# A two-layer graph network: layer 2's attention weights and TensorE sums placed inside the tile in front, with the sums in the residual's PSUM bank

## The chip, the core and the metric

The program runs on one core of a Trainium2 chip. A core has five engines with queues of their own: TensorE (PE; its weight loads are shown as PEld), VectorE (DVE), ScalarE (ACT), GpSimd (POOL) and SyncE (SP). Each works through its own instructions in program order, and engines wait for each other by semaphores. PSUM, the memory that TensorE writes, has eight banks of 512 float32 numbers in each of 128 partitions. The metric is the device time of one execution in microseconds; all arithmetic is in float32.

## The reference, cut to what matters

Two graph attention layers over 10,000 nodes and 170,000 edges (80,000 random ones, their reverses and one loop a node, sorted by destination; the layer then adds a second loop to every node). Layer 1 has 4 heads of 256 columns, layer 2 one head of 768.

```python
def gat_conv(x, edge_index, W, a_src, a_dst, bias, heads, out_ch, concat):
    n = x.shape[0]
    ei = _add_self_loops(edge_index, n)
    src, dst = (ei[0], ei[1])
    xl = (x @ W).reshape(n, heads, out_ch)
    alpha_src = jnp.einsum('nhc,hc->nh', xl, a_src)
    alpha_dst = jnp.einsum('nhc,hc->nh', xl, a_dst)
    e = jax.nn.leaky_relu(alpha_src[src] + alpha_dst[dst], 0.2)
    m = jax.ops.segment_max(e, dst, num_segments=n)
    e = jnp.exp(e - m[dst])
    s = jax.ops.segment_sum(e, dst, num_segments=n)
    alpha = e / (s[dst] + 1e-16)
    msg = xl[src] * alpha[:, :, None]
    out = jax.ops.segment_sum(msg, dst, num_segments=n)
    out = out.reshape(n, heads * out_ch) if concat else out.mean(axis=1)
    return out + bias
...
h0 = x
h = gat_conv(x, edge_index, W1, a_src1, a_dst1, b1, HEADS, HID, True)
h = layer_norm(h, g1, be1)
h = jax.nn.relu(h)
h = h + (h0 @ Wr1 + br1)
h1 = h
h = gat_conv(h, edge_index, W2, a_src2, a_dst2, b2, 1, OUT_DIM, False)
h = layer_norm(h, g2, be2)
h = h + (h1 @ Wr2 + br2)
return h
...
x = _layernorm(x + _L0_gnn_ref(x, edge_index, ...), axis=-1)
```

## The kernel before, in words

Nodes are sorted by degree and cut into 79 tiles of 128 nodes, one node to a partition. A tile has as many *slots* as its largest degree needs: `SLOTS` runs from 8, 9, 10, 11, 11, 11, 12, 12, 12, 13 (five tiles), 14 (five), 15 (eight), 16 (seven), 17 (eight), 18 and 19 (seven each), 20 (six), 21 and 22 (four each), 23, 23, 24, 24, 25, 26, 27 to 41 for the last tile, 1377 in all. In the text n stands for the slots of a tile.

Three stages follow each other. First x @ W1 is written to a table in device memory while the edge lists are prepared. Layer 1 then goes over the tiles, and writes each tile's rows of the layer 2 table (768 columns and two logits) and its h1. Layer 2, `ordered_layer2`, goes over the tiles again; only it is changed.

**The ring.** `Ring.fetch` (called `ring.fetch`) issues one indirect gather on POOL for each slot: 128 table rows of 770 numbers, one to a partition, 394 KB, into one of `RING2` = 40 places used in turn. A place may be filled again when the row in it has been used by DVE and by PE. All gathers go through the helper `gather`, line 409. The loop asks for row k + 40 of its tile right after row k is weighed.

**A tile's work.** `weights_of(t)` (L820 and the helpers `logits`, L454 to L462, and `normalised`, L469 to L475) makes the softmax weights e: adds of logits, maximum and difference on DVE, the exponential on ACT, then the sum, reciprocal and scaling on DVE. It needs every row of the tile to have landed. It is a generator in two halves, before and after the exponential. `sums` (L830 to L837) makes columns 512 to 767 of the weighted sum on PE: a one-row matmul puts the bias in, then for each slot ACT scales the identity by e (a *diagonal*, L836) and PE multiplies it with the row's last 256 columns (L837; a float32 matmul shows as two records). `weigh` (L492) makes columns 0 to 511 with one multiply-add on DVE a slot. `residual(t)` (L846, L848) computes x + h1 @ Wr2 on PE into a tile of two PSUM banks, of which it uses 768 of 1024 columns; `fetch_x` brings h1 (SP, L810) and the rows of x (POOL) for it. The statistics and the scaling by g2 and be2 (`deviation`, L534 to L538, and `scaled`, L547 to L550), the adding of the residual (L874) and the last normalisation follow on DVE; `finish` ends with an ACTIVATE (L884) into the buffer `out`, of which there is one, and a scatter on POOL (L921) sends it to the output rows.

**The order.** The program is emitted by hand in this order, and no scheduler moves it. In the loop for tile t:

- PE and ACT get the sums of tile t, in two halves; between them DVE gets the statistics and scaling of tile t - 1.
- PE gets the residual of tile t + 1 (in the first loop that of tile 0, then `q = product(brT, wr2, C2)`, the shift that br1 makes).
- For k in 0 to n - 1: DVE weighs row k, POOL is given the gather of row k + 40. After row 1 `finish` ends tile t - 1 on DVE and ACT. At n // 2 the inputs of tile t + 2 are asked for. From k = n - 3 (`LEAD` = 3) the two halves of tile t + 1's weights are made, one a row.
- After the last row POOL is given the scatter of tile t - 1.

The last tile, of 41 slots, does not fit in the ring and goes through `attend_parts`: three groups of 13 and 14 rows, all 768 columns on DVE (41 multiply-adds, L492 into `wr`).

PSUM is divided into two buffers `acc` and two `sum` of one bank each, and two residual tiles of two banks: eight banks.

## Time and profile before

| | |
|---|---|
| median of 3 runs | 5635.8 us (5628.9 to 5637.64) |
| the profiled execution | 5634.25 us, span 5632.5 us, mean granted TensorE clock 0.918 |
| first gather of layer 2 | 3570.54 us |
| last scatter | 5627.15 us |
| in 3562 to 5632 us: PE, DVE, ACT, POOL busy | 1674.8, 1636.0, 748.5, 1502.8 us |
| DMA engines in that stretch | busy share 0.90, 316 GB/s |
| POOL over the span | 3411.6 us, 61% |

The profile is one execution. "Busy" counts instructions at work; issuing and waiting are not counted. A timeline row reads: start in us, duration, engine, line, operation, result <- operands, how many merged, and in brackets the idle time of that engine just before, with the instruction or transfer that ended it. A waits row reads: engine, operand and line <- what it waited for: total us, times, longest. `L409 DMA_INDIRECT ring` is POOL's part of one gather; the transfer itself then runs on 16 DMA engines and lands some microseconds after.

### The profile page before, as it was taken

The page shows a single profiled execution, that of the slowest core. Times are in us where ns is not written, and L with a number is a line of the kernel's source. Part 1 is how long each engine was busy: PE and PEld are TensorE (multiplying, and loading weights), DVE is VectorE, ACT ScalarE, POOL GpSimd, SP SyncE. Part 2 cuts the span into 40 slices and gives each one's busy share as a digit, 9 for nine tenths or more (in the row PEclk, how much of TensorE's full clock was granted, in tenths as well). Part 3 has the DMA queues.
Part 4 walks back from the last instruction along what each step waited for, and adds up shares of the span by engine and source line. Part 5 has one row for each costly group of instructions (what it writes and reads, how often), then busy time and mean ns, then how long its engine had stood idle before and what let it go on. Part 6 is the DMA issues. An engine that isn't in the chain of part 4 may idle for free. (4 is left out here: it accounts for less than half of the span.)

```text
span 5632.5 us, 56575 instructions
## 1 busy us (share of the span) xinstructions
PE 4694.2 (83%) x14464; PEld 2762.6 (49%) x14464; DVE 4446.0 (79%) x7881; ACT 3145.5 (56%) x8061; POOL 3411.6 (61%) x3396
## 2 busy tenths in 40 slices
PE   9999997999999998888777654499988888888772
PEld 4444444555555555444444332266556565555551
DVE  5883344788999999999998888388888887877777
ACT  3433444678878888877788766144444343333331
POOL 3446455455556666655655553477777777777773
PEclk9999998999999999999988877799999999888886
DMA  4322427789998999999998876699999999999995
GB/s 155 122 98 80 93 95 263 269 299 327 327 325 324 335 341 332 333 329 326 331 336 320 309 286 225 224 315 330 331 327 332 326 333 324 325 328 330 330 327 163
DMA packets 438659, 1580.90 MB, mean 281 GB/s; under 512 B 102764, under 2 KB 106924, under 8 KB 438327
## 3 DMA queue, kind: packets, MB, share of 16 engines
q0 software_dynamic: 341344, 1400.80, 69.9%
q1 hardware_dynamic: 93168, 170.98, 9.1%
q10 hardware_dynamic: 3814, 5.39, 0.3%
q8 instruction: 122, 2.00, 0.1%
q14 instruction: 211, 1.72, 0.1%
HBM read 1431.10 MB, written 146.19 MB: 280 GB/s over the span
## 5 line engine op out<-in xcount | busy, mean ns | idle before, releaser
L409 POOL DMA_INDIRECT ring<-table,slots x2754 | 2633.6, 956 | 1452.0 <-DVE acc L492 381.5
L492 DVE SCALAR_TENSOR_TENSOR acc<-ring,e,acc 128x256 f32<-128x256 f32 (+1 forms) x2606 | 1609.2, 618 | 134.4 <-PE acc L686 54.5
L481 ACT ACTIVATE ring<-ring,e 128x256 f32<-128x256 f32 x3536 | 1437.1, 506 | 0.0
L488 DVE TENSOR_TENSOR acc<-acc,ring 128x1024 f32<-128x1024 f32 x884 | 1089.1, 1232 | 78.6 <-DVE acc L492 0.9
L837 PE MATMUL sum<-ring,diagonals 128*128 128x256 f32 x2672 | 698.8, 425 | 258.9 <-ACT diagonals L836 256.6
L162 PE MATMUL big<-wr,xT 128*128 128x512 f32 x1896 | 867.4, 616 | 0.7 <-ACT xT L559 0.7
L848 PE MATMUL big<-w,wr 128*128 128x512 f32 (+1 forms) x2528 | 841.0, 485 | 0.0
L162 PE MATMUL big<-w,xT 128*128 128x512 f32 x1896 | 824.8, 597 | 19.1 <-DMA w<-in_W_dram 8.7
L162 PE MATMUL big<-w,hT 128*128 128x512 f32 (+1 forms) x2528 | 833.2, 487 | 1.2 <-ACT hT L559 1.2
L837 PEld LDWEIGHTS sum<-ring,diagonals 128*128 128x128 f32 x2672 | 564.8, 215 | 392.2 <-ACT diagonals L836 296.5
L162 PEld LDWEIGHTS big<-w,hT 128*128 128x128 f32 x2528 | 479.5, 190 | 375.1 <-issue 340.1
L848 PEld LDWEIGHTS big<-w,wr 128*128 128x128 f32 x2528 | 478.4, 189 | 337.0 <-issue 303.2
L162 PEld LDWEIGHTS big<-w,xT 128*128 128x128 f32 x1896 | 362.5, 192 | 478.9 <-issue 461.2
L162 PEld LDWEIGHTS big<-wr,xT 128*128 128x128 f32 x1896 | 371.6, 200 | 441.8 <-issue 440.9
L686 PE MATMUL acc<-ring,diagonals 128*128 128x256 f32 x1248 | 336.0, 430 | 277.8 <-ACT diagonals L681 245.6
L836 ACT ACTIVATE diagonals<-ident,e 128x128 f32<-128x128 f32 x1336 | 420.1, 388 | 124.2 <-PE sum L837 123.0
L884 ACT ACTIVATE out<-wr,less,sd 128x768 f32<-128x768 f32 x79 | 81.1, 1026 | 644.1 <-DMA out_dram<-out,order 556.4
L686 PEld LDWEIGHTS acc<-ring,diagonals 128*128 128x128 f32 x1248 | 269.9, 219 | 338.2 <-ACT diagonals L681 259.9
L634 DVE TENSOR_TENSOR scr<-big,as_b 128x1024 f32<-128x1024 f32 x79 | 96.7, 1225 | 382.3 <-ACT row L631 382.3
L462 ACT ACT_TABLE_LOAD x155 | 198.9, 1283 | 311.1 <-DVE e L461 283.2
L639 POOL TENSOR_TENSOR row<-row,none 128x1024 f32<-128x1024 f32 x79 | 186.9, 2366 | 270.3 <-ACT row L631 269.8
L637 ACT ACTIVATE scr<-scr 128x256 f32<-128x256 f32 x632 | 253.5, 402 | 122.9 <-DVE scr L634 122.9
(171 smaller groups left out, 3938.4 us busy)
## 6 DMA issues: line engine op xcount, KB each, us to landing
ring<-table,slots POOLq DMA_INDIRECT x2754, 5.8
table<-row SPq DMA_DIRECT2D x79, 516.0 KB, 2.9
h_d<-hT SPq DMA_DIRECT2D x79, 512.0 KB, 7.0
wr<-h_d SPq DMA_DIRECT2D x79, 512.0 KB, 6.8
xT<-in_x_cols_dram SPq DMA_DIRECT2D x79, 384.0 KB, 4.3
w<-in_W_dram SPq DMA_DIRECT2D x6, 512.0 KB, 7.3
w<-in_W_dram SPq DMA_DIRECT2D x1, 3072.0 KB, 12.9
wr<-in_Wr_dram SPq DMA_DIRECT2D x1, 3072.0 KB
```

Source lines behind the costliest of these rows:

```text
L162: nc.tensor.matmul(p[:, c:e], aT[:, j, :], w[:, j, c:e], start=(j == 0), stop=(j == k - 1))
L409: nc.gpsimd.indirect_dma_start(out=to, out_offset=None, in_=table, in_offset=bass.IndirectOffsetOnAxis(ap=index, axis=0), **more)
L462: nc.scalar.activation(e, e, AF.Exp)
L481: nc.scalar.activation(row[:, s], row[:, s], AF.Copy, scale=e[:, h:h + 1])
L488: nc.vector.tensor_add(acc[:, :c], acc[:, :c], row[:, :c])
L492: nc.vector.scalar_tensor_tensor(acc[:, s], row[:, s], e[:, h:h + 1], (acc if first is None else first)[:, s], op0=OP.mult, op1=OP.add)
L637: nc.scalar.activation(m[:, s], m[:, s], AF.Copy, accum_out=row[:, C1 + i * H1 + h:C1 + i * H1 + h + 1])
L639: nc.gpsimd.tensor_add(row[:, :C1], row[:, :C1], b1_b)
L686: nc.tensor.matmul(acc[:, c:d], diagonals[:, k * H1 + i, :], ring.slot(FIRST[t] + k)[:, c:d], start=(k == 0 and c % BANK == 0), stop=(k == ...
L836: nc.scalar.activation(diagonals[:, k % G, :], ident, AF.Copy, scale=e[:, k, :])
L837: nc.tensor.matmul(acc, diagonals[:, k % G, :], ring.slot(FIRST[t] + k)[:, ON_PE2:C2], start=False, stop=(k == n - 1))
L848: nc.tensor.matmul(r[:, c:d], hT[:, j, :], wr2[:, j, c:d], start=False, stop=(j == K1 - 1))
```

## The change

Layer 2's loop is written anew with the same operations; helpers are as before.

- The sums on PE become part of `weights_of`: the second half now normalises the weights and then at once makes the tile's diagonals and matmuls. They accumulate into columns 768 to 1023 of the tile's residual, which shares its second bank; so residual(t) has to be issued before. There are no `sum` buffers any more; residual tiles (`big`) become three. Diagonals have `DIAGONALS` = 5 buffers of four instead of two.
- The two halves of tile t + 1's weights are made at row `turn` and three rows later. `turn` is a third of n, or, if more, the row at which the ring has been allowed six rows beyond the end of tile t + 1; at most n - 3.
- `norms` is a generator with the end of tile t - 1 in four pieces, taken in loop t before row 0 (statistics), at row 3 (scaling, residual, statistics), at row 6 (reciprocal, ACTIVATE into `out`) and at row 9 (the scatter on POOL).
- The residual of tile t + 1 is issued at the top of loop t. Residual(0), q and residual(1) come first on PE, ahead of the sums of tile 0; q is added to be2 at the end of loop 0.
- The ring has 38 places instead of 40.

```diff
-RING2 = 40
+RING2 = 38
 LEAD = 3
+DIAGONALS = 5
...
-                tc.tile_pool(name="ps_q2", bufs=2, space=PSUM) as ps_big, tc.manual_schedule():
+                tc.tile_pool(name="ps_q2", bufs=3, space=PSUM) as ps_big, tc.manual_schedule():
...
             def weights_of(t):
...
                 yield e
                 normalised(small, e, H2, t)
+                to = rs[t][:, C2:2 * C2 - ON_PE2]
+                nc.tensor.matmul(to, ones, b2_b[0:1, ON_PE2:], start=False, stop=False, skip_group_check=True)
+                for k in range(n):
+                    if k % G == 0:
+                        diagonals = pool.tile([P, G, P], F32, name="diagonals", bufs=DIAGONALS)
+                    nc.scalar.activation(diagonals[:, k % G, :], ident, AF.Copy, scale=e[:, k, :])
+                    nc.tensor.matmul(to, diagonals[:, k % G, :], ring.slot(FIRST[t] + k)[:, ON_PE2:C2],
+                                     start=False, stop=(k == n - 1), skip_group_check=True)
                 yield
...
+            def norms(t, h, r, means):
+
+                stats = deviation(small, [a for m in means for a in pieces(m, C2 - ON_PE2)])
+                yield
+                scaled(h, means, stats, g2_b, be2_b)
+                nc.vector.tensor_add(h, h, r[:, :C2])
+                mean, inv = deviation(small, pieces(h, C2 // 2))
+                yield
+                nc.vector.reciprocal(inv, inv)
+                less = small.tile([P, 1], F32, name="less")
+                nc.vector.scalar_tensor_tensor(less, mean, -1.0, inv, op0=OP.mult, op1=OP.mult)
+                o = pool.tile([P, C2], F32, name="out")
+                nc.scalar.activation(o, h, AF.Identity, bias=less, scale=inv)
+                yield
+                nc.gpsimd.indirect_dma_start(
+                    out=out, out_offset=bass.IndirectOffsetOnAxis(ap=nodes(t), axis=0),
+                    in_=o, in_offset=None, bounds_check=N - 1, oob_is_err=False)
...
+            rs = {0: residual(0)}
+            q = product(brT, wr2, C2)
+            last = iter(())
...
+            for t in range(NT):
+                n = SLOTS[t]
+                if t + 1 < NT:
+                    rs[t + 1] = residual(t + 1)
+                h = parts[4 + t % 2][:, :C2]
+                if not whole(t):
+                    for _ in last:
+                        pass
...
+                    last = norms(t, h, rs[t], [h])
+                else:
+                    e = (ready or list(weights_of(t)))[0]
                     acc = ps_acc.tile([P, BANK], F32, name="acc")
...
+                    next(last, None)
+                    ready, ahead, turn = [], iter(()), n
+                    if t + 1 < NT and SLOTS[t + 1] + LEAD <= ring.size:
+
                         ahead = weights_of(t + 1)
+                        turn = min(max(n // 3, n + SLOTS[t + 1] + 2 * LEAD - ring.size), n - LEAD)
+                    for k in range(n):
+                        if k in (turn, turn + LEAD):
                             ready += itertools.islice(ahead, 1)
+                        if k in (LEAD, 2 * LEAD, 3 * LEAD):
+                            next(last, None)
                         weigh(acc, ring.slot(FIRST[t] + k), e[:, k], ON_PE2, None if k else b2_b)
                         ring.fetch(FIRST[t] + k + 1 + ring.size)
...
+                    ready += ahead
+                    for _ in last:
+                        pass
+                    if not t:
+                        nc.vector.tensor_add(be2_b, be2_b, q[:, :C2])
+                    last = norms(t, h, rs[t], [acc, rs[t][:, C2:2 * C2 - ON_PE2]])
```

## The prediction

> **What bounds the kernel now.** I read the page's slices and costliest groups first, then the busy times by stage, then GpSimd's waits, and last the timelines of the two ends of layer 2. The page's POOL line and two of its groups:
>
> ```profile
> POOL 3446455455556666655655553477777777777773
> L409 POOL DMA_INDIRECT ring<-table,slots x2754 | 2633.6, 956 | 1452.0 <-DVE acc L492 381.5
> L884 ACT ACTIVATE out<-wr,less,sd 128x768 f32<-128x768 f32 x79 | 81.1, 1026 | 644.1 <-DMA out_dram<-out,order 556.4
> ```
>
> Layer 2 is the last 14 slices, and POOL is flat at 7 there. A gather is 0.95 us busy and has 0.30 us in front of it even where nothing is late, so a 7 is an engine with no free time. The stages say so (us; PE, PEld, DVE, ACT, POOL; clock, DMA share, GB/s):
>
> ```profile
> 3820.00:4020.00 200.00, 186.25 (x651) 121.62 (x650) 174.86 (x376) 80.66 (x195) 153.08 (x155) 0.99 0.94 330
> 5220.00:5420.00 200.00, 155.98 (x541) 110.93 (x540) 156.15 (x300) 73.42 (x189) 151.38 (x159) 0.88 0.93 328
> ```
>
> 155 to 159 gathers and scatters in 200 us are one every 1.26 to 1.29 us. GpSimd's waits between 3620 and 5520 us:
>
> ```profile
> POOL ring L409 <- issue: 111.2, 365, 0.3
> POOL ring L409 <- PE sum L837: 76.4, 239, 2.6
> POOL ring L409 <- DVE acc L492: 47.9, 130, 3.9
> ```
>
> 239 waits on PE of 76.4 us are 0.32 us each: the fixed gap, not PE. Above 0.31 us a gap, all of POOL's waits from 3600 to 5558 us come to about 21.5 us, and most of them are these, at the start:
>
> ```profile
> 3637.93 0.94 POOL L409 DMA_INDIRECT ring<-table,slots  x1 [3.87 <-DVE acc L492]
> 3649.54 0.94 POOL L409 DMA_INDIRECT ring<-table,slots  x1 [9.42 <-DVE e L454]
> 3665.86 0.97 POOL L409 DMA_INDIRECT ring<-table,slots  x1 [2.42 <-DVE acc L492]
> 3775.19 0.94 POOL L409 DMA_INDIRECT ring<-table,slots  x1 [1.95 <-DVE acc L492]
> ...
> 5502.71 0.94 POOL L409 DMA_INDIRECT ring<-table,slots  x1 [0.30 <-DMA ring<-table,slots]
> ...
> 5570.66 1.63 POOL L409 DMA_INDIRECT ring<-table,slots  x1 [12.03 <-DVE wr L492]
> ```
>
> From 3775 to 5558 us POOL sets the pace, and the change leaves it the same 1377 gathers, 79 of x and 79 scatters. So time can only be won before 3775 and after 5558, and lost between. PE's start and DVE's two late waits:
>
> ```profile
> 3605.44 1.19 PE L830 MATMUL sum<-b,ones 1*128 1x256 f32 x2 [44.62 <-DVE ad L820]
> 3613.00 1.02 PE L846 MATMUL big<-wr,ident 128*128 128x512 f32 x2
> 3636.13 1.13 PE L846 MATMUL big<-wr,ident 128*128 128x512 f32 x2 [1.05 <-DVE be L912]
> ```
> ```profile
> 5508.34 0.18 DVE L454 TENSOR_TENSOR e<-ring,ad 128x16 f32<-128x16 f32 x1 [7.00 <-DMA ring<-table,slots]
> 5569.05 0.21 DVE L475 TENSOR_SCALAR e<-e,loops 128x1 f32<-128x1 f32 x1 [19.59 <-ACT e L462]
> ```
> ```profile
> 5566.46 1.03 ACT L884 ACTIVATE out<-wr,less,sd 128x768 f32<-128x768 f32 x1 [18.96 <-DMA out_dram<-out,order]
> ```
>
> PE's residuals stand behind DVE's first weights. At the end DVE waits for the exponential, which stands on ACT behind the output of tile 77; that waits for its one buffer, whose scatter POOL reached only at 5557.6.
>
> **Start: residual and product ahead of the first sums (gain 15 us).** Tile 0's x gather is issued at 3580.6 and lands 11.3 us later; Wr2 and h1 are there. So residual(0) can start at 3592 in place of 3613. Its 11.65 us (3613.00 to 3624.6) plus 2 us for a cold clock give 3605.6. The product of br1 takes 10.5 (its operand is ready at 3602.2): 3616. Residual(1): 3628. The sums of tile 0, 0.65 + 8 x 0.46 us: 3632; of tile 1: 3637. Before, tile 0's statistics began at 3638.5 and tile 1's sums ended at 3652.6. Residual(2) then waits on PE for its buffer, which tile 0's normalisation frees at about 3640 (before: 3652.6 start).
>
> The clock: the first two bias matmuls took 629 and 761 ns against 345 later, hence the 2 us. The Trainium skill, "TensorE: Matmul & The Clock Gate", section on what is actually happening, has the array at half clock for about 3.4 us of activity after idling; that would make it 1.7 us by an estimate from the page, and the wait for residual(2), 3 us, too short to cool it.
>
> DVE per tile is 0.77n + 8.7 us: 14 multiply-adds in 11.04 us at 4719.3, 5.9 us of statistics and scaling, 0.4 for the reciprocal, 2.4 for weights. From 3632 that gives tile starts at 3648, 3664, 3681, 3699, 3716, 3734, 3752 (n = 9, 10, 11, 11, 11, 12, 12); PE's 13 + 0.46n stays ahead of it. The gather that POOL made at 3775.2 is row 125; with 38 slots it is freed by row 3 of the tile begun at 3752, after its scaling, at about 3760. Lead 15 us. Below, 5 (if residual(0) starts no earlier than 3602); above, 20 (nearly all 21.5 us of stalls).
>
> **Output scatter from behind the tile's last gather to its row 9 (gain 18.5 us at the end, costs 2.6 there).** It passes n - 9 gathers on POOL; the finishing ACTIVATE goes from row 1 to row 6. For tile 76's scatter that is 18 gathers, some 22 us, so it has landed before ACT wants the buffer for tile 77. The tail then is: reciprocal at 5547.9, ACTIVATE 1.03, table load 1.28, exponential 0.21, DVE at 5550.5 instead of 5569.05: 18.5 us. Ahead of the last row of tile 77 (POOL at 5502.71) there now stand one more scatter and one more gather of x: 2 x 1.3 us later. Two more multiply-adds after that row, 1.5 us, against a wait of 1.4 us for the deviation at 5521 that goes: 0.1. Between the ends ACT's 556 us on the scatter vanish and return as DVE waiting for gathers: nothing, since POOL paces both. On SP the h1 loads keep their place at n // 2.
>
> **Scatter waiting on POOL for ACT (2 us).** What is queued behind it is every later gather. For n of 20 and more ACT ends 3 us or more before POOL arrives: for n = 26, about 24 us after the preceding tile's last row is issued, against 21 gathers and one x, 27 us. For n of 9 to 11 the diagonals (11 x 0.31) stand ahead of the ACTIVATE, so POOL, which has no backlog there, loses about 2 us once; then it has one. Bounds 0 and 6 (three such tiles).
>
> **Weights at the turn, ring of 38 (2 us).** For n of 19 and more DVE stops at the row where the last row of the next tile is six freed slots back from POOL's limit. POOL may issue that row and six more: its eighth issue is due 8.75 us after the row's. DVE goes on 4.7 to 6.2 us after the row's issue (last row and L454's second piece in the 14 last tiles before: 5502.71 to 5508.34 is 5.6), does 0.85 of logits, 0.35 of reciprocal where the turn is row 6, a multiply-add of 0.77, and POOL follows 0.25 later: at 6.9 to 8.4. So POOL is not held, with 0.3 to 1.8 us to spare. Single gathers landed in 5.2 us (median), one in ten in over 7.1, the latest 9.2; at 9.2 POOL would lose 2.7 us in each of 28 tiles, 75 us. Bounds 0 and 75; I take 2, since the direct pairs all fall inside.
>
> In a sentence apart: the Trainium skill, "DMA: Bandwidth & Descriptors", section on the anatomy of one DMA, fits 2.0 us plus bytes over 436 GB/s, an estimate of 2.9 us for 394 KB; by it six rows would be ample and this term nothing, while the rows above say nearly twice that under this load.
>
> **Other edits (nothing).** Sums behind the residual on PE instead of in front: same matmuls, and PE has 14 us (n = 13) to 44 us free in 200. Diagonals, 5 buffers of 4: all of a tile up to n = 20 without waiting for PE. The exponential no longer stands behind the finishing ACTIVATE: its 152 us on DVE become waits for gathers, except at the start, where they are in the 15. A sum in the residual's bank: both are read only after PE is through with that tile; with no pair of engines in one bank at once it costs neither way, and if the shared tile made PE wait, the 44 us would cover 5 us a tile of the wide ones.
>
> **Sum.** -15 + 2 - 18.5 + 2.6 + 0.1 + 2 = -26.8 us. The profiled execution took 5634.25 us (span 5632.5 and 1.75 around it): 5607.5, span 5605.7. It lies 1.5 us under the median of 5635.8, so 5609 for a median; I say 5608.
>
> **Rivals.**
> 1. *The start is bound by its loads.* Residual(0) starts no earlier than DVE did; for it speaks that DVE waited until 3604 for vectors, against it that residual(0) uses none of them. The 15 falls to 0 to 5: 5619 to 5624.
> 2. *Six slots are too few: slower.* Place: row "turn" of the 28 tiles with n of 19 or more, POOL waiting for DVE's multiply-add, DVE for the landing. It turns the sign once 28 tiles lose 1.4 us each more (39 us), which is a gather landing 1.7 to 3 us later than in the pairs; at 9.2 us landing, 5608 + 73 = 5681. For it: one in ten beyond 7.1 us. Against it: POOL's issue rate, and so the load, is as before.
> 3. *The pace is POOL's and both ends stay.* The last exponential finds another late wait, or the lead at the start is spent at the pauses of tiles 1 to 10: 5625 to 5640.
>
> **How the numbers follow.** Forecast 0.58, its own range 5596 to 5617; rival 1 0.12; rival 3 0.11; rival 2 0.19. A measurement of this kernel tells about 0.2%, 11 us, from no change, so faster means under 5624.5: 0.58 + 0.12 = 0.70; the same is rival 3 and the mild end of 2, 0.14; slower, past 5647, 0.16. The range goes from 5594 to 5645 and leaves out the worse part of rival 2.
>
> **What the profile after would show.** First residual matmul on PE near 3592, not 3613; POOL's waits over 0.5 us before 3800 down from 21 to about 8 us; POOL at 155 to 159 in 200 us in the middle; no ACT wait on the output scatter; the last exponential within 3 us of its logits. Wrong would be gaps of over 0.5 us in front of L409, by DVE acc L492, once a tile after 4300.

## The result, and the profile after

| | median | range | ratio to before, 95% interval |
|---|---|---|---|
| before, 4 runs | 5634.73 us | 5628.9 to 5637.64 | |
| after, 4 runs | 5604.41 us | 5600.86 to 5607.76 | 0.9947, 0.993 to 0.9965 |

The change takes 30 us off; the forecast was 5608 us. The profiled execution of after took 5606.97 us, with a span of 5605.1. So the sum came out. Its terms did not: two errors of about 15 us in it cancel, which is luck. On another chip the sign did not hold either: there the same kernel was 0.5% slower. What follows takes the terms apart.

The page of after, GpSimd's slices and its costliest group:

```profile
POOL 2446465455555666655665554377777777777774
L410 POOL DMA_INDIRECT ring<-table,slots x2754 | 2620.8, 952 | 1445.1 <-DVE acc L493 393.3
```

GpSimd is as flat in layer 2 as before, but its gathers are a little shorter: 2620.8 us in all, 12.8 less than before. The busy times by stage (us; PE, PEld, DVE, ACT, POOL; clock, DMA share, GB/s):

```profile
3820.00:4020.00 200.00, 189.50 (x669) 123.94 (x668) 173.34 (x379) 82.64 (x194) 152.47 (x157) 1.00 0.94 337
5220.00:5420.00 200.00, 147.21 (x504) 103.30 (x504) 147.70 (x284) 67.39 (x174) 150.31 (x156) 0.85 0.92 325
5430.00:5510.00 80.00, 54.07 (x186) 38.57 (x185) 53.14 (x102) 25.25 (x67) 55.10 (x57) 0.81 0.85 289
```

In the early stretch GpSimd issues 157 in 200 us where it issued 155. In the late ones it falls behind: 156 for 159, and 57 in the 80 us from 5430, where before had 64:

```profile
5430.00:5510.00 80.00, 54.05 (x192) 38.32 (x190) 55.09 (x108) 25.36 (x65) 60.70 (x64) 0.84 0.93 325
```

Layer 2 is a fixed list of 1377 gathers, so the plainest way to see where time was won is to compare the clock of the same gather in both traces. The table gives the lead of after over before: issue time before minus issue time after. (Tiles are counted from 0. Six tiles have 14 slots, not five as in the list ahead of the prediction; with six, the tiles are 79 and the slots 1377.)

| last gather of | lead of after | what happened since the line above |
|---|---|---|
| first gather of layer 2 | -1.0 us | layer 1 ended 1 us later in this execution |
| the 126th (tile 11) | 10.1 | start: +11 |
| tile 71 (n = 23) | 26.3 | middle: +16 |
| tile 77 (n = 27) | 12.4 | late tiles: -14 |
| end of the span | 27.4 | tail: +15 |

The start and the tail that the forecast lived on are there, each smaller than forecast. Two that it did not have in this size, +16 and -14, nearly cancel.

**Start.** TensorE's first matmuls of layer 2:

```profile
3593.14 2.05 PE L847 MATMUL big<-wr,ident 128*128 128x512 f32 x2 [31.33 <-DMA wr<-in_x_dram,order]
3594.97 8.78 PE L850 MATMUL big<-w,wr 128*128 128x512 f32 x16
```

The residual of tile 0 starts at 3593 as soon as its x rows are there. It runs cold: 2.05 us for the first two, 1.02 before, and 8.78 for the next sixteen, 7.03 before. The granted clock is 0.50 from 3590 to 3594 us and 1.00 from 3604 on.

**Late tiles.** Tile 77's diagonals, and what stands behind them on ScalarE:

```profile
5500.03 8.17 ACT L835 ACTIVATE diagonals<-ident,e 128x128 f32<-128x128 f32 x27 [3.02 <-DVE e L473]
5508.22 1.28 ACT L539 ACT_TABLE_LOAD   x1
5509.52 0.29 ACT L539 ACTIVATE sd<-mv,eps 128x1 f32<-128x1 f32 x1
```

VectorE and GpSimd at the same place:

```profile
5509.84 0.16 DVE L550 RECIPROCAL sd<-sd 128x1 f32<-128x1 f32 x1 [3.81 <-ACT sd L539]
```
```profile
5514.71 0.94 POOL L410 DMA_INDIRECT ring<-table,slots  x1 [5.51 <-PE big L836]
```

Since the sums are no longer split, all 27 diagonals go out in one piece ahead of the square root of tile 76's deviation. VectorE, which needs that root to scale, stands 3.81 us; it weighs no rows meanwhile, no slots come free, and GpSimd stops for 5.51 us. The last row names TensorE, but the place that this gather fills (38 gathers back: row 3 of tile 77, the first that is weighed behind the scaling) is left by TensorE at 5504.3 and by VectorE at 5514.0. From 4700 us on there are six stops over 1 us in front of the ring's gathers, the last four 2.06, 2.83, 4.82 and 5.51 us. Before had none between 4700 and 5550 us.

The root is not all of it. In front of the last three stops VectorE stands 1.73, 2.54 and 3.81 us for it, 8.1 of their 13.2 us. The rest of VectorE's delay lies at the turn, where it waits for rows to land with five rows of its own tile still to weigh (three before):

```profile
5495.92 0.17 DVE L455 TENSOR_TENSOR e<-ring,ad 128x6 f32<-128x6 f32 x1 [8.86 <-DMA ring<-table,slots]
```

And the ring has two places less, which at one issue in 1.25 us are 2.5 us of cover a tile, an estimate as large as the waits for the root. No run has the changed kernel with 40 places.

Of the -14, counted between the same two gathers, 8.7 us are stops (the last, 5.51 us, lies behind tile 77's last gather and so in the tail), 2.6 are two more issues of GpSimd in that stretch (163 for 161) and the rest are gathers that last longer.

**Tail.** The last group's exponential of the last tile:

```profile
5541.69 0.21 DVE L476 TENSOR_SCALAR e<-e,loops 128x1 f32<-128x1 f32 x1 [1.10 <-ACT e L463]
```

It used to wait 19.59 us and now waits 1.10. From here to the end it is 63.4 us in both.

### The profile page after: what moved, and what is told of

It reads as the page before. It is cut to its first block, busy times and chain, and to the rows that moved or that the text cites. A ratio compares the mean times of both kernels' runs of the same rounds, so it can differ in the third digit from the quotient of the medians.

```text
span 5605.1 us, 56678 instructions
## 1 busy us (share of the span) xinstructions
PE 4697.6 (84%) x14464; PEld 2749.3 (49%) x14464; DVE 4424.7 (79%) x7882; ACT 3138.7 (56%) x8061; POOL 3395.6 (61%) x3396
## 5 line engine op out<-in xcount | busy, mean ns | idle before, releaser
L410 POOL DMA_INDIRECT ring<-table,slots x2754 | 2620.8, 952 | 1445.1 <-DVE acc L493 393.3
L850 PE MATMUL big<-w,wr 128*128 128x512 f32 (+1 forms) x2528 | 865.8, 496 | 0.0
L836 PE MATMUL big<-ring,diagonals 128*128 128x256 f32 x2672 | 656.0, 407 | 171.2 <-ACT diagonals L835 138.5
L836 PEld LDWEIGHTS big<-ring,diagonals 128*128 128x128 f32 x2672 | 540.4, 205 | 283.2 <-ACT diagonals L835 186.7
L835 ACT ACTIVATE diagonals<-ident,e 128x128 f32<-128x128 f32 x1336 | 398.5, 387 | 126.5 <-DVE e L473 117.2
L539 ACT ACTIVATE sd<-mv,eps 128x1 f32<-128x1 f32 x237 | 69.8, 294 | 591.7 <-DVE mv L537 591.2
```

Of the source, the lines that this page charges most:

```text
L410: nc.gpsimd.indirect_dma_start(out=to, out_offset=None, in_=table, in_offset=bass.IndirectOffsetOnAxis(ap=index, axis=0), **more)
L835: nc.scalar.activation(diagonals[:, k % G, :], ident, AF.Copy, scale=e[:, k, :])
L836: nc.tensor.matmul(to, diagonals[:, k % G, :], ring.slot(FIRST[t] + k)[:, ON_PE2:C2], start=False, stop=(k == n - 1), skip_group_check=True)
L850: nc.tensor.matmul(r[:, c:d], hT[:, j, :], wr2[:, j, c:d], start=False, stop=(j == K1 - 1 and (d < C2 or not whole(t))), skip_group_check= ...
```

## The middle: gathers that are held

Nothing was forecast for the middle, yet 16 us were won there, where GpSimd had hardly waited. The gathers themselves became shorter. From 3830 to 5280 us the mean of all GpSimd's DMA instructions fell from 0.980 to 0.965 us (1128 and 1140 of them): of the gathers, of table rows and of x, 77 lasted more than 1.05 us before, 31.9 us longer than 0.95 in sum, and 35 after, 14.2 us longer. Between the two gathers that bound the +16 (1185 instructions of GpSimd in both), the instructions are 18.0 us shorter in sum and the gaps 1.8 us longer. The kernel before, VectorE and GpSimd in one tile (rows of other kinds left out):

```profile
3943.89 1.02 DVE L550 SCALAR_TENSOR_TENSOR wr<-wr,sd,be 128x768 f32<-128x768 f32 x1
3944.08 1.65 POOL L409 DMA_INDIRECT ring<-table,slots  x1 [0.30 <-PE sum L837]
...
3947.11 0.71 DVE L492 SCALAR_TENSOR_TENSOR acc<-ring,e,b 128x512 f32<-128x512 f32 x1
3947.28 1.35 POOL L409 DMA_INDIRECT ring<-table,slots  x1 [0.31 <-issue]
```

Both long gathers begin while VectorE runs an instruction that reads two tensors from SBUF (scaling: `wr` and `be`; the tile's first multiply-add: the ring's row and the bias). Both end 0.81 to 0.82 us after that instruction ends. The other multiply-adds read one operand from SBUF and one from PSUM, and no gather is long beside them.

The order matters by chance. Before, scaling came 3.2 us ahead of the first multiply-add. A held gather sets GpSimd's 1.25 us beat, and 3.2 us later the multiply-add began 0.17 us ahead of a gather and held it too: 49 long gathers fell on that multiply-add and 28 on scaling, and in all 28 tiles where scaling held one, the multiply-add did as well. With scaling moved to row 3, behind the first multiply-add, no tile has both: 25 and 10.

The Trainium skill, "SBUF — State Buffer", section "Who interferes with whom", says that a VectorE instruction with two SBUF inputs contends with a GpSimd instruction that reads SBUF, that the ports they share are an exclusive lock, and that the order of issue decides who blocks. These rows agree, for the case in which VectorE was first.

## The experiments

They ran in three groups, each on one chip and beside runs of the kernel before there. On the chip of the g runs the kernel before takes 5638.39 us, much as in the first runs. On those of the e and the f runs it takes 5952.33 and 5952.32 us. In the trace of e2, which differs from it in a buffer alone, layer 2 begins 22 us later than in the first trace and takes 288 us longer. I call the two kinds free and held chips; why is told under f1. Times are compared within a group, unless the text says otherwise.

### e1: the start alone (held chip)

```diff
+                if not t:
+                    rs[0] = residual(0)
+                    q = product(brT, wr2, C2)
                 if last:
                     h, r, means = last
...
-                    if not t:
-                        rs[0] = residual(0)
-                        q = product(brT, wr2, C2)
-                    elif t + 1 < NT:
+                    if t and t + 1 < NT:
```

> The kernel before, with only TensorE's start of the change: residual(0) and the product of br1 ahead of the first sums. Nothing is left out of the computation. Forecast's theory (the start alone is worth a lead of 10 to 15 us, and GpSimd keeps it to the end): 5634.7 - 10 to 15 = 5620 to 5625; first residual matmul near 3593 us, GpSimd's waits over 0.5 us between 3600 and 3800 down from 20 to 8 us or less. Rival (the lead is given back, since GpSimd paces the middle): lead at row 125 of 10 us or so, but 5632 to 5636 in all.

Measured: 5937.36 us against 5952.33, ratio 0.9972 (0.9957 to 0.9986), 15 us. That is in the difference what was forecast for the term, though on this chip the interval is wide, 8 to 26 us. The trace is sharper: against e2, which has the old start, the gathers of e1 lead by 10.4 us from tile 5 and by 10.9 at tile 16, the size of after's own lead at the start. The rival (bound by loads, 0 to 5) is out.

### e2: two buffers for the output alone (held chip)

```diff
-                    o = pool.tile([P, C2], F32, name="out")
+                    o = pool.tile([P, C2], F32, name="out", bufs=2)
```

> The kernel before with two buffers for the output instead of one: ACT's last ACTIVATE of a tile no longer waits for the scatter of the tile in front, and nothing else is moved. Nothing is left out. Forecast's theory (of that wait only the 19 us at the last tile count, the other 537 are covered by GpSimd): 5634.7 - 16 to 19 = 5616 to 5619, the lead of the gathers in the middle between -2 and +2 us until row 1300. Rival (the wait also paces the middle through the exponential behind it): 5600 to 5612. Rival (the wait comes back as a wait for gathers): 5632 to 5636.

Measured: 5932.14 us, ratio 0.9967 (0.9957 to 0.9978), 20 us. The tail can be had without moving the scatter: ScalarE only has to stop waiting for the buffer.

### e3: the scaling behind the first multiply-adds, alone (held chip)

```diff
-                    scaled(h, means, stats, g2_b, be2_b)
-                    nc.vector.tensor_add(h, h, r[:, :C2])
-                    mean, inv = deviation(small, pieces(h, C2 // 2))
+                    def middle(h=h, r=r, means=means, stats=stats):
+                        ...
...
+                        if last and k == LEAD:
+                            middle()
+                            if t + 1 < NT:
+                                rs[t + 1] = residual(t + 1)
```

> The kernel before with the scaling of tile t-1 moved from ahead of row 0 of tile t to row 3 (its last ACTIVATE follows two rows later, the residual of tile t+1 follows the scaling on TensorE); weights, sums, ring and scatter stay. Nothing is left out. Theory of the long gathers (a gather that begins while VectorE runs an instruction with two SBUF operands is held until that ends; with the scaling in front, the multiply-add that reads the bias always falls on the start of a gather, with the order changed it does not): of the gathers of over 1.05 us between 3830 and 5280 us, 77 before, 30 to 45 are left, the lead grows by 13 to 18 us there, 5617 to 5622 in all. Rival (the lead in the middle comes from weights made earlier or from the earlier scatter): 70 to 80 long gathers, 5632 to 5638.

The residual and the last ACTIVATE move along. Measured: 5937.39 us, ratio 0.9972 (0.9961 to 0.9982), 15 us. Long gathers from 3830 to 5280 us: 37 (13.2 us longer), against 58 and 52 (23.6 and 19.3 us) in e1 and e2, which have the old order. The order is what thins them out. That the 15 us come from them is not shown by this run, since GpSimd does not set the pace on this chip: it is busy 133 to 135 us in every 200, where 152 is full.

### e4: the bias of columns 0 to 511 by TensorE (held chip)

```diff
+                    nc.tensor.matmul(acc, ones, b2_b[0:1, :ON_PE2], start=True, stop=True)
...
-                        weigh(acc, ring.slot(FIRST[t] + k), e[:, k], ON_PE2, None if k else b2_b)
+                        weigh(acc, ring.slot(FIRST[t] + k), e[:, k], ON_PE2)
```

> The kernel before with the bias of columns 0 to 511 put into the accumulator by a one-row TensorE matmul, so that the first multiply-add of a tile reads PSUM and one SBUF row instead of two SBUF operands. Nothing is left out. Theory of the long gathers: the 49 long ones at that multiply-add, 16.7 us in 3830 to 5280, go; those at the scaling (28, 15.3 us) stay or change by some: lead in the middle 8 to 18 us, 5614 to 5625 in all. Rival (these gathers are long for another reason, such as traffic on the DMA engines): 70 to 80 long gathers, 5633 to 5638.

Measured: 6016.97 us, ratio 1.0101 (1.0083 to 1.0118): 65 us slower, where 10 to 20 faster was expected. The mechanism did what it should: of 29 long gathers none falls on a first multiply-add any more, all 29 on scaling. But one matmul more a tile, about 1 us of TensorE, cost 0.8 us a tile. VectorE's multiply-adds, of which the first in a tile now needs that matmul, wait for TensorE's sums 27 times between 3820 and 5600 us, 166 us in all. So on this chip TensorE is behind, and gathers are not the currency; whether the 65 us are the matmul's time or the new wait was not separated.

### f1: the changed kernel itself on a held chip

> The changed kernel itself, once more beside the kernel before, as the yardstick of the three runs that follow it. Where layer 2 is paced by GpSimd's issues, as in the two profiles read so far (150 to 153 us of every 200): 0.993 to 0.9965 of the time before, minus 20 to minus 40 us, with some 35 gathers longer than 1.05 us between the clocks 3830 and 5280 where the kernel before has some 77. Where layer 2 runs as it did on the chip of the first four runs (GpSimd 133 of every 200, TensorE's sums stopping several times a tile), two theories part. If the gains of the start, the tail and the order add up there as they came singly (15, 20 and 15 us), 0.9916, minus 50 us. If that chip is paced by TensorE's sums, all of a tile's sums in one go ahead of the residual must themselves change the pace, and the difference is well outside minus 40 to minus 60 us in one direction or the other.

Measured: 5986.44 us against 5952.32, ratio 1.0053 (1.0028 to 1.0078): **34 us slower**. TensorE in one tile there:

```profile
4419.73 2.75 PE L850 MATMUL big<-w,wr 128*128 128x256 f32 x12
4422.41 0.69 PE L831 MATMUL big<-b,ones 1*128 1x256 f32 x2
4423.03 0.70 PE L836 MATMUL big<-ring,diagonals 128*128 128x256 f32 x2
4424.18 0.38 PE L836 MATMUL big<-ring,diagonals 128*128 128x256 f32 x1 [0.44 <-issue]
4426.98 0.59 PE L836 MATMUL big<-ring,diagonals 128*128 128x256 f32 x1 [2.42 <-issue]
4429.08 1.44 PE L836 MATMUL big<-ring,diagonals 128*128 128x256 f32 x3 [1.51 <-issue]
```

Matmuls that come every 0.215 us suddenly come one at a time, and the profile names nobody who would have ended the idle time in front of them ("issue"); instruction by instruction, weight loads included, the steps are 1.40 us. In layer 2 of f1, 191 TensorE instructions without any wait of their own start 0.9 us or more after the one in front, 170 of them 1.38 to 1.41 us after it. In e1, e2 and e4 there are 157 to 167 of them, in f2 and f3 201 and 230, in e3 and f4 39 and 95 (the number in the expectation of g1 does not hold for these two). Counted otherwise, as TensorE's idle times over 0.4 us from 3700 to 5500 us that the profile puts down to nobody, they come to 193 to 318 us in all eight held runs, e3 with 271 among them. In the first traces of before and after, and in all four g runs, there is not one by either count. In f1 they form 64 stops, so one in most tiles, after 20 us (median) of unbroken matmuls. On the free chips unbroken stretches of 22 us (median) pass without a stop. What makes TensorE step is not known; see g1.

The stops alone do not say why the change loses. Against e2 (the other held chip; layer 2 begins 1.4 us earlier there), f1's gathers lead by 3 us at tile 5, 9 at tile 40 and 6 at tile 52. Then they lose: 10 us behind at tile 62, 15 at tile 64, 41 at tile 76. So it is again the tiles with long rows. A wait that grew, f1 (total us, times, longest):

```profile
DVE sd L550 <- ACT sd L539: 118.3, 11, 12.7
```

and after on the first chip:

```profile
DVE sd L550 <- ACT sd L539: 23.1, 12, 3.8
```

ScalarE's diagonals have five buffers of four; when TensorE is stopped, the rest of them wait for it, and the square root waits behind them: 12.7 us at the longest. With four more of which the releaser is not recorded, fifteen of VectorE's scalings from 5337 us on stand 7 to 12.7 us, and GpSimd's last four stops in front of ring gathers are 6.4, 11.3, 11.6 and 11.6 us. It is the late tiles' loss of the first chip, larger: there too the place that the last three gathers wait for is that of row 3. It is not the whole loss. The 16 us between tile 52 and tile 62 go before 5270 us, ahead of the first of the fifteen waits (5337 us), and were not traced. The gains of e1, e2 and e3 did not simply add up here, so of the two theories the second came true in its number; that it is the sums in one go that change the pace is left to f3.

### f2: the turn with 3 slots of slack instead of 6 (held chip)

```diff
-                        turn = min(max(n // 3, n + SLOTS[t + 1] + 2 * LEAD - ring.size), n - LEAD)
+                        turn = min(max(n // 3, n + SLOTS[t + 1] + LEAD - ring.size), n - LEAD)
```

> The changed kernel with its turn reckoned for 3 slots of slack instead of 6, so that in the tiles with long rows the next tile's weights and sums begin 3 rows later; nothing else differs. The second rival of the forecast, made true by hand. If the slots of the ring bound the late tiles (theory: the loss of 11 us after tile 71 is slots that come free too late), GpSimd has 3 x 1.25 = 3.75 us less cover in each tile from about n = 19 on, and is held 2 to 3.5 us in some 15 of them: 30 to 55 us slower than the changed kernel (ratio to before 0.999 to 1.005), the stops being in the profile as waits for TensorE's sum or VectorE's multiply-add in front of the ring's gathers. If that loss comes from ScalarE's diagonals alone and the six slots had more than they needed, within 6 us of the changed kernel.

Measured: 5973.4 us, ratio 1.003 (1.0015 to 1.0045): 13 us below f1, with intervals that overlap. Neither number was expected. Turning later did not hurt: apart from its layer 2 beginning 5 us earlier it is level with f1 up to tile 40, and gains some 11 us by tile 64. On a chip where GpSimd is busy 126 to 136 us in every 200, this says nothing on whether six slots were needed where it has no time to spare.

### f3: in the late tiles, the sums behind the deviation again (held chip)

```diff
-            def weights_of(t):
+            def weights_of(t, late=False):
...
                 normalised(small, e, H2, t)
+                if late:
+                    yield
                 to = rs[t][:, C2:2 * C2 - ON_PE2]
...
+                        late = n >= 22 and n - turn < 11
+                        ahead = weights_of(t + 1, late)
```

The deferred part is issued after the next tile's statistics, and the residual after it.

> The changed kernel, but in tiles of 22 rows and more that turn late, ScalarE's diagonals and TensorE's sums of the next tile are issued behind the deviation of this one (and ahead of the next residual), so that the square root no longer stands behind 8 us of diagonals. Theory (the order on ScalarE costs the late tiles 11 us and the tail 3.5): the waits of VectorE's scaling for ScalarE's square root (23 us in 12 waits) shrink to under 5 us, and GpSimd's last three stops (2.8, 4.8 and 5.5 us) with them: 6 to 12 us faster than the changed kernel. Rival (the stops come from the scaling's pause at row 3 and from slots that the sums hold): the sums come later, their slots come free later, and the time stays within 3 us or rises by up to 10.

Measured: 5958.99 us, ratio 1.0014 (1.0002 to 1.0026): 27 us below f1, intervals just apart. f3 and f1 are within 1 us of each other from tile 5 to tile 52; then f3 gains, 6 us by tile 64 and 23 by tile 76. Of the fifteen long waits for the square root five are left, 56.7 us, not under 5 as expected: they lie between 5331 and 5477 us, ahead of the tiles of 22 rows where the deferring begins, and behind these there is none; the reciprocal of the last normalisation waits 26.8 us in five instead. As 6 of the 27 us are there before the deferring begins, putting the diagonals and sums back behind the root in the late tiles returned some 20 of the 34 us, more than the 6 to 12 expected. The rival is out on this chip.

### f4: no two operands from SBUF in the rows' loop (held chip)

```diff
+                accs[t] = ps_acc.tile([P, BANK], F32, name="acc")
+                nc.tensor.matmul(accs[t], ones, b2_b[0:1, :ON_PE2], start=True, stop=True)
+                if t >= FOLD:
+                    for c in range(0, C2, BANK):
+                        d = min(C2, c + BANK)
+                        nc.tensor.matmul(rs[t][:, c:d], ones, be2_b[0:1, c:d], start=False, stop=(d < C2),
+                                         skip_group_check=True)
...
-                scaled(h, means, stats, g2_b, be2_b)
-                nc.vector.tensor_add(h, h, r[:, :C2])
+                folded = t >= FOLD and whole(t)
+                scaled(h, means, stats, g2_b, r[:, :C2] if folded else be2_b)
+                if not folded:
+                    nc.vector.tensor_add(h, h, r[:, :C2])
```

> The changed kernel without VectorE instructions in the rows' loop that read two operands from SBUF: the layer's bias is put into the sum of columns 0 to 511 by a one-row matmul on TensorE, and the shift of the second norm is folded into the residual's bank by two more, so that scaling reads wr and the bank, and the addition of the residual goes. Theory (a gather that is issued while such an instruction runs is held until its end): the gathers longer than 1.05 us go from some 35 to under 5 between the clocks 3830 and 5280 and the mean gather to 0.950 us, worth 14 us there and some 20 over layer 2; VectorE loses 0.95 us of addition a tile besides: 15 to 25 us faster than the changed kernel where GpSimd's issues pace layer 2. Rival (the length of the gathers is the queue's, as the DMA rings are 94% busy): the long gathers stay, within 5 us. Second rival: three more one-row matmuls a tile, 1.5 us of TensorE, come onto the path as they did when the bias alone was moved in the kernel before (65 us slower there, on a chip where GpSimd was not the pace): slower by 10 us or more.

Measured: 6040.48 us, ratio 1.016 (1.0131 to 1.019): 54 us above f1, the second rival, as in e4. Yet of GpSimd's 940 DMA instructions from 3830 to 5280 us not one lasts over 1.05 us, and the mean is 0.951: the cause of the long gathers is settled. (Only the long instructions with two operands from SBUF are gone; the adds of the logits, 0.2 us, still have two.) What they are worth needed a chip or a kernel with TensorE out of the way.

### g1 and g2: before and after with a quarter of the residual product (free chip)

```diff
-                    for j in range(K1):
+                    for j in range(1):
```

> The kernel before with a quarter of the residual product of layer 2: of the four 128-row pieces of h.T W_res only the first is multiplied in, the loads stay, so its output lacks the rest; TensorE has some 7.7 us less to do a tile. Theory: on the chips of the eight runs so far layer 2 is slower than in the two profiles read first because TensorE is held there: its instructions without any wait come at steps of 1.40 us, 157 to 230 of them in layer 2 of each run (none in the two first profiles), always after some 20 us of unbroken matmuls. With 7.7 us less a tile these steps go to under 20, GpSimd is busy 150 to 153 of every 200 us again, and the time is 5590 to 5640 us. Rival: the steps come from something else (loads, instruction supply, the chip's memory); they stay, and the time stays above 5850 us. Where the chip is of the first kind, there are no steps in either case and the time is 5590 to 5640 us; the comparison of the next two runs with this one then stands on its own.

> The changed kernel with the same quarter of the residual product, to be read against the kernel before made light in the same way. Theory (the change gains where GpSimd's issues pace layer 2, and loses only where TensorE is held): 20 to 35 us below the light kernel before, that is the 30 us of the first chip less some of the 10 at the start, as the residual ahead of the first sums is now 6 us instead of 14 in both. Rival (the sums in one go, ahead of the deviation, cost time on these chips whatever TensorE's load, as the 34 us by which the changed kernel was slower there): 10 us below to 40 us above the light kernel before.

Measured: 5621.65 and 5599.65 us; ratios to the whole kernel before 0.9974 (0.9963 to 0.9985) and 0.9937 (0.992 to 0.9954). They came up on a chip without the steps, so the light kernel says nothing on what causes them, and that stays open. The pair still stands: light after is 22 us below light before. By the leads of its gathers 3 of the 11 us at the start remain (0.1 against -2.9 us at the first gather, as the two layer 1s ended differently). The middle gives 14 us, with 86 long gathers against 29: GpSimd's instructions are 23.5 us shorter, its stops 9.9 us longer. The late tiles cost 6, and the tail brings 15. So with less for TensorE to do the middle and the tail stay and the late loss is under half. The waits for the root in front of the last three stops are as long as in after (1.47, 2.55 and 3.75 us), so they alone do not set that loss.

### g3: the light changed kernel without two operands from SBUF (free chip)

> The changed kernel without two-operand reads from SBUF in the rows' loop (bias of columns 0 to 511 and the second norm's shift put in by TensorE), with the same quarter of the residual product, so that TensorE has room for its added one-row matmuls. What a held gather costs, where GpSimd paces the layer: no gather over 1.05 us, as in the full kernel of this form (0 of 940), the mean gather 0.95 us, and by the theory that the time follows GpSimd's issues 14 to 25 us below the light changed kernel. Rival (a held gather only shifts GpSimd inside slack that it has anyway): within 5 us of it.

Measured: 5574.76 us, 25 us below g2. The ring's gathers from 3830 to 5280 us in g2:

```profile
L410 POOL DMA_INDIRECT ring<-table,slots x1019 | 978.8, 961 | 320.5 <-issue 100.6 <-PE big L836 61.8 <-DVE acc L493 46.8
```

and in g3:

```profile
L410 POOL DMA_INDIRECT ring<-table,slots x1029 | 974.6, 947 | 323.7 <-issue 98.6 <-PE big L843 57.9 <-DVE acc L493 53.5
```

961 ns against 947, no gather over 1.05 us, and a lead over g2 that grows evenly: 4 us at tile 13, 10 at tile 40, 19 at tile 71, 26 at the end (layer 2 began 1.4 us earlier). Where GpSimd's issues set the pace, a held gather costs what it is held. VectorE is also spared an addition, but that hardly counts: of the 23.1 us gained between the first and the last gather of the ring, 21.9 are shorter instructions of GpSimd (1533 in both) and 1.2 are shorter gaps between them.

### g4: the start, the two outputs and the order, without the early sums (free chip)

The diffs of e1, e2 and e3 together, on the kernel before.

> The kernel before, whole, with the three parts of the change that do not move the sums: the first residual ahead of the first sums, two tiles for the output, and the scaling at row 3 instead of ahead of row 0. The sums stay where they were, behind the deviation, in a bank of their own, with 40 slots. On the chips of the eight runs so far, singly 15, 20 and 15 us faster than before, while the whole change was 34 us slower. Theory (the early sums are what costs there): 40 to 50 us faster than the kernel before (ratio 0.9915 to 0.9935). Rival (the parts share one gain, as TensorE sets the pace in between): 15 to 25 us. Second rival (the scaling at row 3, or the two outputs, brings the loss together with another part): slower than before. On a chip where GpSimd paces the layer: 40 to 50 us as well, as each part was reckoned there at 13 to 19 us.

Measured: 5589.56 us against 5638.39, ratio 0.992 (0.9904 to 0.9937): **49 us faster**, as the three added up. The change as it was made got 30 on the first chip. The lead over before, read as above, against the first trace of before (the chips differ or may differ, their kernels before by 4 us):

| last gather of | after | g4 |
|---|---|---|
| tile 13 | 9.6 | 12.7 |
| tile 40 | 20.0 | 24.3 |
| tile 71 | 26.3 | 32.4 |
| tile 77 | 12.4 | 32.9 |
| end of the span | 27.4 | 48.7 |

Start, middle and tail are all there without the early weights and sums; what goes missing is the loss. The middle is again the length of GpSimd's instructions: 20.1 of the 20.6 us between the gathers that bound it. The 80 us from 5430 in g4, by the columns above:

```profile
5430.00:5510.00 80.00, 58.64 (x207) 41.41 (x205) 62.44 (x114) 23.88 (x64) 60.80 (x64) 0.87 0.93 319
```

64 issues in 80 us, as before, for 57 in after. GpSimd's waits on TensorE from 5200 to 5520 us, after (total us, times, longest):

```profile
POOL ring L410 <- PE big L836: 25.6, 44, 5.5
```

and g4:

```profile
POOL ring L409 <- PE sum L837: 14.9, 49, 0.3
```

49 waits of 0.3 us are the fixed gap in front of every gather: no stop is left. Yet VectorE waits for a root here too, and longer, that of the last normalisation, in tile 76:

```profile
5457.53 0.16 DVE L889 RECIPROCAL sd<-sd 128x1 f32<-128x1 f32 x1 [5.24 <-ACT sd L538]
```

There are 52 such waits over 1 us, 161 us in all. They stop nobody, as every place is left at least 2.3 us before GpSimd fills it again (gathers into the places of tile 72 to row 9 of tile 77). In after, where VectorE also waits at the turn and the ring is two places shorter, nothing is left over. So a wait for the root costs only what the ring does not cover, and which of the three (turn, root, ring) takes how much of the 14 us stays open on a free chip.

The three parts alone beat both kernels on a free chip. On a held chip each of them was 15 to 20 us faster; together they were not run there.

## Why the prediction was right, and where its steps failed

- **The total** (5608 forecast, 5604 measured): right, and partly for the reasons given. Start and tail together were put at a gain of 33.5 us (15 and 18.5) and gave some 26; the terms between were put at a loss of 6.7 and gave a gain of 2, as +16 and -14. That these cancel is luck.
- **Start, 15 us:** 11, confirmed alone by e1's trace (10.4 to 10.9) and in g4 (12). The step was right, rival 1 wrong: TensorE's first residual matmul is at 3593.14. The gain lies in GpSimd's waits: those over 0.5 us between 3600 and 3800 fell from 21.6 to 10.7 us, where 8 was forecast. Mis-sized was the chain behind the residual. Its eighteen cold matmuls took 2.8 us more than warm ones, not 2, and tile 0's sums ended at 3633.8, not 3632. The sum let VectorE decide when row 125's place comes free, with TensorE ahead of it; by its own figures TensorE needs longer for a tile of under 14 rows (13 + 0.46n against 0.77n + 8.7). VectorE left that place at 3755.5 and TensorE at 3761.6; the gather went out at 3765.0, forecast 3760, behind GpSimd's own issues. And the 3 us that were "too short to cool" TensorE, 3.46 in the event, did cool it: residual(2) took 1.21 and 8.65 us for the 1.02 and 7.03 of a warm one, at a granted clock of 0.83 from 3642 to 3652 us.
- **"So time can only be won before 3775 and after 5558", as POOL sets the pace between:** the step that failed. It took GpSimd's issue as a constant, 0.95 + 0.30 us, while the row of before already said 956 ns in the mean for gathers of 950, and 974 from 3830 to 5280 us. An engine that sets the pace is worth a look at the spread of its instructions, not only at its waits. The scaling's move to row 3 had no term at all.
- **Scatter waiting on POOL, +2:** GpSimd's waits in front of the output scatter are the fixed gap; none of the 2 us is seen.
- **Weights at the turn, +2, with rival 2 beyond it:** GpSimd does stop in late tiles, and its lead falls by 14 us, but not as the step reckoned. That step followed one row, "turn", with the gather's landing and the logits behind it. The stops are a few rows on, at the scaling of row 3, where VectorE, late already from the turn, waits for a root that stands behind up to 27 diagonals. The prediction priced the diagonals at nothing, "all of a tile up to n = 20 without waiting for PE": it asked what they wait for, not what waits behind them on ScalarE. The waits for the root are 8.1 of the 13.2 us of the last three stops. f3 shows on a held chip that the order in the late tiles costs some 20 us there; on a free chip the share of the order, of the turn and of the two places was not separated.
- **Output scatter, 18.5 at the end and 2.6 ahead:** 15 at the end, and the 2.6 is there, in the late tiles' -14. The wait it was to remove fell from 19.59 to 1.10 us, "within 3 us of its logits" as forecast. g4 has 15.8, so the 3.81 us wait for the root is not the whole of the missing 3.5; the rest was not traced.
- **What would show it wrong,** gaps over 0.5 us by VectorE's multiply-add "once a tile after 4300": only a handful of such gaps, so rightly not fired. "No ACT wait on the output scatter" did not come true: 21 such waits are left, 117 us, the last at 4147 us, in place of 65 with 556; they cost nothing, as GpSimd has no gap over 0.4 us between 3726 and 4710 us.
- **Rival 2's side:** the sign did turn, on a held chip, in about the place it named (late tiles, behind the early weights and sums). Instead of late gathers it was in part ScalarE's queue behind a stopped TensorE; the loss ahead of tile 62 is not explained.

## What to carry to other kernels

Work moved earlier on one engine is work put ahead of something on that engine: before costing a moved block at nothing, list what stands behind it in its queue in the tile where it is longest (here a 0.3 us square root behind 8 us of diagonals), who waits for that, and how much of the wait the buffers in between cover. When an engine's issues set the pace, look at its longest instructions and what runs on the other engines while they last; two-operand reads from SBUF on VectorE cost some 20 us here beside GpSimd's gathers, and a reordering can win or lose that by accident. Try the parts of a change one by one: here three of them gave 49 us, and what is left, the weights and sums that the change was named for with the shorter ring, took some 20 back.

## What the runs showed of the hardware

- A GpSimd gather issued while VectorE runs one of the two instructions with two large SBUF operands (0.7 and 1.0 us) ends 0.81 to 0.82 us after that instruction, in a few cases up to 0.89, and is up to 1.74 us long instead of 0.95; with neither in the loop, none of GpSimd's 940 DMA instructions on one chip (f4) and none of 1147 on another (g3) lasted over 1.05 us.
- On two chips TensorE's instructions stepped at 1.40 us once in most tiles; layer 2 of the kernel before with two outputs (e2) took 288 us longer there than that of the kernel before on the first chip. The granted clock in the six microseconds of one such stop is 0.72 (f1; the columns are those above), which does not explain five matmul records in that time:

```profile
4423.00:4429.00 6.00, 1.70 (x5) 1.06 (x5) 3.64 (x14) 1.25 (x2) 2.35 (x3) 0.72 0.88 339
```

- The Trainium skill, "TensorE: Matmul & The Clock Gate", section "What's actually happening", knows two rates, full and half. The 1.40 us steps are beyond both: half rate would bring 0.43 us for the 0.215 of these matmuls, by an estimate from the row of f1.
